# A modulated layer norm split so that its first product does not wait for the inverse root, with a re-planned instruction order, in an eight-block attention and FP4 kernel

## The chip, the cores and the metric

The kernel runs on one core of one Trainium2 chip. The metric is the device time of one execution in microseconds (us), the median of three runs. The engines are called PE (TensorE, matrix multiply; PEld is its weight load), DVE (VectorE), ACT (ScalarE), POOL (GpSimd) and SP (SyncE, which issues the DMA transfers).

## The reference

The input x has 8 batch elements of 1024 tokens by 128 features, all float32. A small table c (8x128) gives every batch element six modulation rows of 128: shift, scale and gate for the attention part (sa, ca, ga) and for the feed-forward part (sb, cb, gb).

```
mod = (silu(c) @ wmod).reshape(8, 6, 1, 128)
sa, ca, ga, sb, cb, gb = mod[:, 0], ..., mod[:, 5]
ga, gb: magnitude at least 0.25, sign kept
h = layernorm(x) * (1 + ca) + sa
x = x + ga * attn(h)
h = layernorm(x) * (1 + cb) + sb
x = x + gb * ffn(h)
```

`attn` has six layers. Each is a layer norm with weights, linear attention in 8 heads of 16 (softmax of q over the head's features, softmax of k over the tokens, context = k^T v, out = q context), a product with wo plus bias, the residual, then a second layer norm, a 128-to-512 product, a leaky ReLU, a 512-to-128 product and the residual. `ffn` is a gated unit whose three products take inputs rounded to a 4-bit grid in blocks of 16: silu(gate) * up, 128 to 352, then back to 128. `layernorm` alone, without weights, is (x - mean) / sqrt(var + 1e-5).

## The kernel before, in words

**Tiling.** One batch element is a "block" b. Its 1024 tokens lie on 128 partitions as 8 chunks of 128 features, so x of a block is a tile of 128 x 1024. Work goes by halves h of four chunks (128 x 512, one PSUM bank). Four lanes (`LANES = 4`, lane = b % 4) hold the buffers of four blocks in flight; blocks 4 to 7 take over the lanes of 0 to 3. All weights stay in SBUF.

**Order.** The kernel does not emit instructions as it describes them. [...] `Plan.order` (line 143) then plays a schedule over all engines: it takes, again and again, the step that can start earliest, ties broken by the length of the work behind it plus a "lead". Leads are set per block and stage in `LEAD` (from line 291) and altered at planned times by `TURNS` (from line 302). `LAT` (line 87) is what passes between a step's end and its readers' start on each engine, `mm`, `move`, `vec`, `act` and `pool2` (lines 217 to 243) give durations. The steps are emitted in that order, with the order on each engine fixed, so a planned duration that is off costs nothing by itself, but can place an instruction ahead of one that is ready earlier.

Into a gap of PE that the planner foresees (over `GAP` 0.6 us, half of that while it holds PE to be cold) it puts fillers, `warm` (line 1348), matmuls of the identity that nobody reads. Until `COLD` us of planned time it charges matmuls double; for a run of fillers this is decided once, at the run's start. A PSUM bank is claimed by a step only when everything is ready that any later user of the same bank needs and that was recorded before: a transpose whose eviction needs `cols` (the norm weights as columns, copied on DVE at line 515) is planned after that copy.

**The norm.** `layernorm` (line 614) is used for the plain norms of every layer (through `normed`, line 909; tiles named `_a` and `_m`) and for the two modulated norms of a block (`modulated_norm`, line 887; tiles `_i` for the first, `_f` for the second). Per half:

- four batch statistics (line 630) and four aggregates (line 636) on DVE give mean and variance (`mv`);
- ACT makes a first inverse root by Ln and Exp (lines 650, 655);
- three DVE operations of 4 elements (lines 660, 665, 670) refine it by one Newton step into `rstd`, a fourth (line 676) makes `shift` = -mean * rstd;
- the centred, scaled x is written by DVE for the first `HV` chunks (line 682, one tensor_scalar with two pointers per chunk) and by ACT for the rest (line 689, scale and bias as pointers).

`modulated_norm` calls it with HV = 2 of 4 for the first norm of a block and HV = 0 for the second, then multiplies the half by 1 + scale on DVE (line 893, one operation of 128 x 512) and adds the shift row on POOL (line 901, the same size).

What follows: the first modulated norm writes x of lane b, which the first layer's norm reads. There PE transposes the half (line 708), ACT evicts it with the norm weights (line 918) to xT, and PE multiplies it with wk (line 938) and wq (line 985). The other matmuls named below are the attention's (lines 1048, 1057, 1082, 1115), the two products of a layer's feed-forward part (lines 1161 and 1178) and those of `ffn` (line 1222 gate and up, line 1278 transposes, line 1302 down). The second modulated norm writes h, which is rounded to the grid (`fp4`, lines 736 to 781: five DVE operations, one on ACT, one on POOL) and transposed for line 1222. `w2g` (line 1130) is a POOL multiply of the last layer.

Of the kernel before, what the change touches and what calls it, by code (L numbers as in the profile page):

```python
# [83 lines left out]
class Plan:  # L84


    LAT = {"PE": 0.31, "ACT": 0.14, "DVE": 0.125, "POOL": 0.04, "SP": 2.0}
    SEE = {"PE": 0.015, "ACT": 0.0, "DVE": 0.0, "POOL": 0.1, "SP": 0.0}

    GAP, BRINK, COLD = 0.6, 0.15, 7.5  # L90
# [126 lines left out]
def vec(n):  # L217

    return 0.065 + n * 1.043e-3
# [16 lines left out]
def mm(n):  # L236

    return 0.01 + n * 1.66e-3


def move(kb):

    return max(0.45, kb * 4.0e-3)
# [6 lines left out]
def kernel(  # L250
# [53 lines left out]
        (45, [(0, 2, 1600), (3, 0, -324)]),  # L304
        (60, [(1, 1, -935)]),
        (75, [(0, 3, 1449), (1, 1, 557), (3, 1, 592)]),
        (90, [(3, 1, 2100)]),
        (120, [(3, 2, 2464), (3, 3, 2879)]),
        (135, [(0, 3, 3161)]),
        (150, [(1, 1, 2636)]),  # L310
        (165, [(1, 2, 3857)]),
        (195, [(0, 4, 1947)]),
        (210, [(1, 3, 1937)]),
        (225, [(0, 4, 2875), (0, 6, 2412), (0, 7, 99)]),
        (240, [(2, 1, -1301), (3, 3, 1394)]),
        (255, [(0, 5, 2591), (1, 3, 3015), (1, 4, -653)]),
        (270, [(3, 4, 2428)]),
        (345, [(0, 6, 2433), (4, 0, -1503)]),
        (390, [(1, 4, -2461)]),
        (405, [(3, 6, -3105)]),  # L320
        (435, [(1, 4, -3419)]),
        (450, [(3, 6, -3090)]),
        (465, [(2, 2, 551), (2, 4, -3123), (3, 6, -3105)]),
        (510, [(4, 1, -3111)]),
        (525, [(3, 6, -3271)]),
        (540, [(3, 6, -3110)]),
        (600, [(3, 7, 2098)]),
        (615, [(2, 4, -3534)]),
        (630, [(2, 6, -2208), (5, 1, 1840)]),
        (660, [(5, 1, 1745)]),  # L330
        (690, [(5, 1, 2562)]),
        (720, [(4, 3, -2144)]),
        (750, [(2, 6, -2203)]),
        (780, [(2, 6, -2201), (2, 7, -2144), (4, 3, -2142), (5, 4, -2397)]),
        (810, [(2, 7, -2186)]),
        (825, [(3, 7, -2164), (4, 3, -1269)]),
        (840, [(3, 7, -2468)]),
        (870, [(3, 7, -340)]),
        (885, [(3, 7, -553), (4, 4, 939), (4, 5, 1955)]),
        (915, [(5, 4, -1086), (6, 2, -534)]),  # L340
        (945, [(4, 6, 1221)]),
        (975, [(4, 7, -240), (7, 1, -1371)]),
        (990, [(6, 3, 282)]),
        (1005, [(4, 7, -743), (5, 4, -650)]),
        (1035, [(4, 7, -1539), (5, 5, -1458)]),
        (1050, [(5, 5, -591), (6, 3, 867), (6, 4, 1080), (7, 2, 307)]),
        (1095, [(6, 4, -754)]),
        (1110, [(6, 4, -1551)]),
        (1125, [(4, 7, -4373), (6, 4, -758)]),
        (1140, [(6, 5, -1624)]),  # L350
        (1200, [(5, 7, -1877)]),
        (1215, [(6, 5, -185), (7, 4, -2011)]),
        (1230, [(6, 5, -1795)]),
        (1245, [(6, 6, -373), (7, 5, -366)]),
        (1260, [(6, 6, -371), (7, 5, -372)]),
        (1275, [(6, 6, -365), (7, 5, -367)]),
        (1305, [(6, 7, -440), (7, 6, -443)]),
        (1320, [(7, 6, 40)]),
        (1335, [(4, 7, -2064), (5, 7, -2271), (6, 7, -2282), (7, 6, 278), (7, 7, 207)]),
# [254 lines left out]
    def layernorm(ln, dst, src, h, n, HV=HC // 2):  # L614
# [7 lines left out]
        def s(c):  # L622
            return chunks(half(src, h))[:, c, :]

        def d(c):
            return chunks(half(dst, h))[:, c, :]

        for c in range(HC):
            add(
                "DVE", 0.197, lambda c=c: nc.vector.bn_stats(stats.ap()[:, c, :], s(c)),  # L630
                r=at(src, h)[c * H // HC :][:1], w=[stats[c]],
            )

        def moments():
            for c in range(HC):
                nc.vector.bn_aggr(mv.ap()[:, c, :], stats.ap()[:, c, :])  # L636

        add("DVE", HC * 0.067, moments, r=[stats], w=[mv])
# [4 lines left out]
        def var():  # L643
# [28 lines left out]
        )  # L672

        add(
            "DVE", 0.07,
            lambda: nc.vector.scalar_tensor_tensor(z(), mean(), -1.0, y(), ALU.mult, ALU.mult),  # L676
            r=[mv, rstd], w=[shift], port=True,
        )
# [8 lines left out]
        def apply_s():  # L687
# [9 lines left out]
            w=[high] if HV else [low, high],  # L697
        )
        if HV:
            add("DVE", HV * 0.256, apply_v, r=[*at(src, h), mv, rstd], w=[low], port=True)  # L700
# [14 lines left out]
    def fp4(src, parts, ncol, n, i, last="POOL"):  # L715
# [13 lines left out]
        def each(t):  # L729
# [50 lines left out]
            last, (vec if last == "DVE" else pool2)(ncol),  # L780
# [106 lines left out]
    def modulated_norm(ln, dst, src, mod, n, name, HV):  # L887

        for h in range(H):
            layernorm(ln, dst, src, h, name, HV)  # L890
            add(
                "DVE", vec(HW),
                lambda h=h: nc.vector.tensor_tensor(
                    chunks(half(dst, h)), chunks(half(dst, h)),
                    over(mod.ap()[:, n + 1, :], HC), ALU.mult,
                ),
                r=[mod[n // 3]], w=at(dst, h), port=True,
            )
            add(
                "POOL", 1.2,  # L900
# [509 lines left out]
```

## Time and profile before

| what | us |
|---|---|
| median of 3 runs | 1406.71 |
| lowest, highest run | 1405.73, 2585.54 |
| profiled execution, its own time | 1406.12 |
| its span, first to last instruction | 1404.4 |
| granted PE clock, mean | 0.999 |

Two of the three runs are within 0.1% of each other; one took 2585.54 and does not move the median. The span leaves out 1.7 us of the profiled execution.

| stretch, us | length | PE busy | DVE busy | ACT busy | POOL busy |
|---|---|---|---|---|---|
| 0 to 50 | 50 | 44.97 | 44.06 | 33.23 | 13.15 |
| 50 to 350 | 300 | 300.00 | 229.52 | 208.56 | 36.90 |
| 350 to 400 | 50 | 48.80 | 40.08 | 35.85 | 10.54 |
| 400 to 750 | 350 | 349.88 | 287.67 | 242.37 | 59.62 |
| 750 to 800 | 50 | 48.36 | 37.96 | 29.39 | 9.27 |
| 800 to 1300 | 500 | 499.54 | 413.19 | 367.48 | 88.67 |
| 1300 to 1405 | 105 | 99.75 | 90.03 | 66.11 | 29.58 |

How to read it: busy time is the union of an engine's instructions in the stretch. Ends of matmuls are modelled and matmuls overlap, so a busy PE may still be held up for moments; the distance from one matmul's start to the next tells more. A group's mean duration is that of one instruction by itself; in a row, DVE and ACT instructions overlap, and one more costs less than the mean. An f32 matmul leaves two records, a transpose one. In a timeline row the two first numbers are the start and the length, xN is the number of instructions merged, and the bracket at the end says how long the engine had been idle before and what ended that.

### The profile page before, as it was taken

To read this page: it belongs to the slowest core of one execution; us is meant where nothing else is said; L and a number is where in the kernel's file an instruction comes from. 1 tells how busy PE (TensorE), PEld (TensorE's weight loads), DVE (VectorE), ACT (ScalarE), POOL (GpSimd) and SP (SyncE) were. 2 spreads that over 40 slices of the span, in tenths; PEclk is the share of its full clock that TensorE was granted. 3 is DMA by queue.
4 is the path that set the end of the run, shared out by engine and by line. 5 is a ranking of instruction groups with operands and counts; after the bars stand their busy time and mean duration, and the time that the engine had idled before them with its cause. 6 is when DMAs were issued, how large, how long until landed. Compare 5 with 4: busy or idle time off the path is not lost.

```text
span 1404.4 us, 26348 instructions
## 1 busy us (share of the span) xinstructions
PE 1391.3 (99%) x9181; PEld 1116.3 (79%) x9181; DVE 1142.5 (81%) x4506; ACT 983.0 (70%) x2292; POOL 247.7 (18%) x216
## 2 busy tenths in 40 slices
PE   8999999999999999999999999999999999999998
PEld 6788779688768888688788778788787787887887
DVE  8998668487798687899667899988876748879897
ACT  6777666766686686767666668876776757777774
POOL 2211001001122020312101122211210101212232
PEclk9999999999999999999999999999999999999999
DMA  7100000000000000100000000000000000000001
GB/s 218 47 1 1 2 1 1 0 1 1 17 12 16 1 2 1 42 16 13 2 0 1 16 13 16 1 16 1 1 1 1 1 1 1 2 1 1 9 17 38
DMA packets 16293, 18.79 MB, mean 13 GB/s; under 512 B 1584, under 2 KB 10392, under 8 KB 16160
## 3 DMA queue, kind: packets, MB, share of 16 engines
q1 hardware_dynamic: 16160, 17.10, 3.9%
q8 instruction: 73, 1.20, 0.4%
q14 instruction: 60, 0.49, 0.1%
HBM read 12.88 MB, written 4.22 MB: 12 GB/s over the span
## 4 chain that ended last, share of the span: by engine, by line
PE 88%; DVE 7%; ACT 2%; SPq 1%; DMA 1%; issue 1%; POOL 0%; POOLq 0%; ACTq 0%; DVEq 0%
PE ps L1178 22%; PE ps L1161 22%; PE ps L708 11%; PE ps L1048 6%; PE ps L938 5%; PE ps L1115 5%; PE ps L985 5%; PE ps L1222 5%; PE ps L1302 3%; PE ps L1278 1%; SPq L417 1%; DVE x L1100 1%; PE ps L1082 1%; PE ps L1057 1%; DMA x<-in_L_attn_x_dram 1%; DVE stats_m L630 1%
## 5 line engine op out<-in xcount | busy, mean ns | idle before, releaser
L1161 PE MATMUL ps<-xT_m,w_sb 128*128 128x512 f32 x768 | 352.0, 595 | 0.3 <-ACT xT_m L918 0.3
L1161 PEld LDWEIGHTS ps<-xT_m,w_sb 128*128 128x128 f32 x768 | 137.6, 191 | 128.8 <-issue 95.6
L1026 POOL TENSOR_TENSOR q<-q,qsum 128x512 f32<-128x512 f32 x96 | 102.4, 1075 | 709.2 <-DVE qsum L1021 377.2
L1100 DVE TENSOR_TENSOR x<-ps,x 128x512 f32<-128x512 f32 x192 | 129.7, 680 | 105.2 <-PE ps L1178 81.1
L985 PEld LDWEIGHTS ps<-wq_sb,xT_a 128*128 128x128 f32 x768 | 96.4, 192 | 26.3 <-issue 18.9
L689 ACT ACTIVATE xh_a<-x,shift_a,rstd_a 128x128 f32<-128x128 f32 x192 | 83.6, 487 | 34.6 <-DVE shift_a L676 33.4
L1115 PEld LDWEIGHTS ps<-m,qT 128*128 128x128 f32 x768 | 92.3, 192 | 11.1 <-issue 4.3
L985 PE MATMUL ps<-wq_sb,xT_a 128*128 128x128 f32 x768 | 98.8, 275 | 0.0
L1178 PEld LDWEIGHTS ps<-w_sb,hT_D 128*128 128x128 f32 x640 | 86.6, 192 | 14.3 <-issue 11.2
L938 PE MATMUL ps<-xT_a,wk_sb 128*128 128x512 f32 x192 | 96.1, 597 | 1.6 <-ACT xT_a L918 1.6
L1178 PE MATMUL ps<-w_sb,hT_C 128*128 128x128 f32 x640 | 97.6, 275 | 0.0
L1178 PE MATMUL ps<-w_sb,hT_E 128*128 128x128 f32 x640 | 97.6, 275 | 0.0
L1178 PE MATMUL ps<-w_sb,hT_B 128*128 128x128 f32 x640 | 97.6, 275 | 0.0
L1178 PE MATMUL ps<-w_sb,hT_D 128*128 128x128 f32 x640 | 97.5, 275 | 0.0
L1115 PE MATMUL ps<-m,qT 128*128 128x128 f32 x768 | 95.9, 275 | 0.1
L689 ACT ACTIVATE xh_m<-x,shift_m,rstd_m 128x128 f32<-128x128 f32 x192 | 81.8, 487 | 17.8 <-DVE shift_m L676 17.6
L1048 PEld LDWEIGHTS ps<-k,xh_a 128*128 128x128 f32 x768 | 90.4, 192 | 4.2 <-issue 2.2
L1048 PE MATMUL ps<-k,xh_a 128*128 128x128 f32 x768 | 93.4, 275 | 0.0
L650 ACT ACTIVATE rstd_a<-mv_a,eps 128x4 f32<-128x4 f32 x96 | 28.1, 296 | 88.2 <-DVE mv_a L636 84.1
L630 DVE BATCH_NORM_STATS2 stats_a<-x 128x6 f32<-128x128 f32 x384 | 84.9, 279 | 3.5 <-POOL x L901 1.7
L918 ACT ACTIVATE xT_m<-ps,cols 128x512 f32<-128x512 f32 x96 | 72.1, 776 | 20.1 <-PE ps L708 20.0
L1178 PEld LDWEIGHTS ps<-w_sb,hT_B 128*128 128x128 f32 x640 | 84.5, 192 | 1.0 <-issue 1.0
(181 smaller groups left out, 3229.8 us busy)
## 6 DMA issues: line engine op xcount, KB each, us to landing
x<-in_L_attn_x_dram SPq DMA_DIRECT2D x16, 256.0 KB, 3.4
out_dram<-x SPq DMA_DIRECT2D x14, 256.0 KB, 2.0
w_sb<-in_L_attn_w_dram SPq DMA_DIRECT2D x12, 256.0 KB, 4.4
mod<-mod_d SPq DMA_DIRECT2D x8, 256.0 KB
mod<-mod_d SPq DMA_DIRECT2D x4, 128.0 KB
out_dram<-x SPq DMA_DIRECT2D x4, 128.0 KB
wmod_b<-in_L_wmod_dram SPq DMA_DIRECT2D x1, 384.0 KB, 4.1
wk_sb<-in_L_attn_wk_dram SPq DMA_DIRECT2D x6, 64.0 KB, 4.1
```

Of the source, the lines that this page charges most:

```text
L630: "DVE", 0.197, lambda c=c: nc.vector.bn_stats(stats.ap()[:, c, :], s(c)),
L689: nc.scalar.activation(d(c), s(c), AF.Identity, bias=shift.ap()[:, c : c + 1], scale=rstd.ap()[:, c : c + 1],)
L708: nc.tensor.transpose(t.ap()[:, c * P : (c + 1) * P], chunks(half(src, h))[:, c, :], ident)
L918: lambda t=t, h=h: nc.scalar.activation(half(xT, h), t.ap(), AF.Identity, bias=col(params + 1, l), scale=col(params, l),),
L938: lambda tk=tk, h=h: nc.tensor.matmul(tk.ap(), wk_sb[:, l, :], half(xT, h), start=True, stop=True),
L985: nc.tensor.matmul(tq.ap()[:, c * D : (c + 1) * D], half(xT, h)[:, c * P : (c + 1) * P], wq_sb[:, l, :], start=True, stop=True,)
L1026: lambda h=h, hs=hs: nc.gpsimd.tensor_tensor(heads(half(q, h)), heads(half(q, h)), each(qsum.ap()[:, hs]), ALU.mult),
L1048: nc.tensor.matmul(tc_.ap()[:, :D], chunks(xh.ap())[:, c, :], chunks(k.ap())[:, c, :], start=(c == 0), stop=(c == C - 1),)
L1100: lambda: nc.vector.tensor_tensor(half(x, h), t.ap(), half(x, h), ALU.add),
L1115: nc.tensor.matmul(to.ap()[:, c * D : (c + 1) * D], half(qT, h)[:, c * P : (c + 1) * P], m.ap(), start=True, stop=True,)
L1161: lambda th=th, h=h, j=j: nc.tensor.matmul(th.ap(), w1_sb[:, l, j * P : (j + 1) * P], half(xmT, h), start=True, stop=True,),
L1178: nc.tensor.matmul(ty.ap()[:, c * D : (c + 1) * D], hidden(j)[:, c * P : (c + 1) * P], w2g.ap()[:, j, :] if l == L - 1 else w2_sb[:, l, j, :],
```

## The change

Four things change.

1. *The norm is cut in two.* `moments` ends with `rstd`; the fourth small operation (`shift`) is made only for the plain norms. These keep DVE for two chunks and ACT for two.
2. *The modulated norm has a body of its own.* Per chunk, DVE makes (x - mean) * (1 + scale) in one scalar_tensor_tensor, which needs the mean and not the inverse root. Then, in blocks whose norm is not "quick", ACT multiplies each chunk by rstd and POOL adds the shift row to the half, as before. In a quick norm, DVE multiplies by rstd and adds the shift row in a second scalar_tensor_tensor per chunk, and neither ACT nor POOL takes part. Quick are the first norm of block 0 and the second norm of block 7.
3. *Durations in the planner.* `LAT` of SP is 2.6 for 2.0, `COLD` 11.5 for 7.5, `mm` and `move` have other coefficients, and three POOL steps are longer. None of them is an instruction.
4. *Leads.* `TURNS` is a new table of 53 rows for 57; `LEAD` is kept.

```diff
-    LAT = {"PE": 0.31, "ACT": 0.14, "DVE": 0.125, "POOL": 0.04, "SP": 2.0}
+    LAT = {"PE": 0.31, "ACT": 0.14, "DVE": 0.125, "POOL": 0.04, "SP": 2.6}
...
-    GAP, BRINK, COLD = 0.6, 0.15, 7.5
+    GAP, BRINK, COLD = 0.6, 0.15, 11.5
...
-    return 0.01 + n * 1.66e-3
+    return 0.0115 + n * 1.654e-3
...
-    return max(0.45, kb * 4.0e-3)
+    return max(0.45, kb * 3.6e-3)
...
-        (45, [(0, 2, 1600), (3, 0, -324)]),
-        (60, [(1, 1, -935)]),
...
+        (45, [(0, 2, 1600)]),
+        (60, [(1, 1, -1561)]),
...
-    def layernorm(ln, dst, src, h, n, HV=HC // 2):
+    def moments(ln, src, h, n, shifted=False):
...
-        add(
-            "DVE", 0.07,
-            lambda: nc.vector.scalar_tensor_tensor(z(), mean(), -1.0, y(), ALU.mult, ALU.mult),
-            r=[mv, rstd], w=[shift], port=True,
-        )
+        if shifted:
+            add(
+                "DVE", 0.07,
+                lambda: nc.vector.scalar_tensor_tensor(
+                    z(), mean(), -1.0, y(), ALU.mult, ALU.mult
+                ),
+                r=[mv, rstd], w=[shift], port=True,
+            )
+        return mv, rstd, shift
+
+    def layernorm(ln, dst, src, h, n):
+
+
+        HV = HC // 2
+        mv, rstd, shift = moments(ln, src, h, n, True)
...
-            last, (vec if last == "DVE" else pool2)(ncol),
+            last, vec(ncol) if last == "DVE" else pool2(ncol) * 1.15,
...
-    def modulated_norm(ln, dst, src, mod, n, name, HV):
+    def modulated_norm(ln, dst, src, mod, n, name, quick):
+
+
 
         for h in range(H):
-            layernorm(ln, dst, src, h, name, HV)
-            add(
-                "DVE", vec(HW),
-                lambda h=h: nc.vector.tensor_tensor(
-                    chunks(half(dst, h)), chunks(half(dst, h)),
-                    over(mod.ap()[:, n + 1, :], HC), ALU.mult,
-                ),
-                r=[mod[n // 3]], w=at(dst, h), port=True,
-            )
-            add(
-                "POOL", 1.2,
-                lambda h=h: nc.gpsimd.tensor_tensor(
-                    chunks(half(dst, h)), chunks(half(dst, h)),
-                    over(mod.ap()[:, n, :], HC), ALU.add,
-                ),
-                r=[mod[n // 3]], w=at(dst, h),
-            )
+            mv, rstd = moments(ln, src, h, name)[:2]
+
+            def chunk(t, c, h=h):
+                return chunks(half(t, h))[:, c, :]
+
+            def first(cs, chunk=chunk, mv=mv):
+                for c in cs:
+                    nc.vector.scalar_tensor_tensor(
+                        chunk(dst, c), chunk(src, c), mv.ap()[:, c, 0:1],
+                        mod.ap()[:, n + 1, :], ALU.subtract, ALU.mult,
+                    )
+
+            def second(cs, chunk=chunk, rstd=rstd):
+                for c in cs:
+                    nc.vector.scalar_tensor_tensor(
+                        chunk(dst, c), chunk(dst, c), rstd.ap()[:, c : c + 1],
+                        mod.ap()[:, n, :], ALU.mult, ALU.add,
+                    )
+
+            def scaled(cs, chunk=chunk, rstd=rstd):
+                for c in cs:
+                    nc.scalar.mul(chunk(dst, c), chunk(dst, c), rstd.ap()[:, c : c + 1])
+
+            Q = HC // H
+            for q, (s, d) in enumerate(zip(at(src, h), at(dst, h))):
+                cs = range(q * Q, (q + 1) * Q)
+                add(
+                    "DVE", Q * vec(D), lambda f=first, cs=cs: f(cs),
+                    r=[s, mv, mod[n // 3]], w=[d], port=True,
+                )
+                if quick:
+                    add(
+                        "DVE", Q * vec(D), lambda f=second, cs=cs: f(cs),
+                        r=[rstd, mod[n // 3]], w=[d], port=True,
+                    )
+                else:
+                    add("ACT", Q * act(D, 1), lambda f=scaled, cs=cs: f(cs), r=[rstd], w=[d])
+            if not quick:
+                add(
+                    "POOL", 1.3,
+                    lambda h=h: nc.gpsimd.tensor_tensor(
+                        chunks(half(dst, h)), chunks(half(dst, h)),
+                        over(mod.ap()[:, n, :], HC), ALU.add,
+                    ),
+                    r=[mod[n // 3]], w=at(dst, h),
+                )
...
-                "POOL", pool2(NJ * D) + 0.1,
+                "POOL", pool2(NJ * D) + 0.28,
...
-                    "POOL", pool2(HW) + 0.2,
+                    "POOL", pool2(HW) + 0.33,
...
-        modulated_norm(ln, hq, x, mod, 3, f"f{b}", 0)
+        modulated_norm(ln, hq, x, mod, 3, f"f{b}", b == B - 1)
...
-        modulated_norm(ln, x, x0s[b], mod, 0, f"i{b}", HC // 2)
+        modulated_norm(ln, x, x0s[b], mod, 0, f"i{b}", b == 0)
```

## The prediction

> **What bounds the kernel now.** I read the page's busy shares first, then the busy time of the engines by stretch, then the same table for the filler matmuls alone, then the timeline around the places where TensorE is not busy.
>
> ```profile
> PE 1391.3 (99%) x9181; PEld 1116.3 (79%) x9181; DVE 1142.5 (81%) x4506; ACT 983.0 (70%) x2292; POOL 247.7 (18%) x216
> ...
> PE   8999999999999999999999999999999999999998
> ```
>
> TensorE (PE) is busy for 1391.3 of 1404.4 us. The next engine, VectorE (DVE), has 262 us free. So only two things can shorten the run: less work on TensorE, or fewer moments in which it waits. Part of its busy time is no work of the reference: the planner puts "warm" matmuls (line 1350) into gaps that it foresees. By stretch, those alone (us of window, PE busy and count, PEld busy and count, granted clock, DMA):
>
> ```profile
> 0.00:50.00 50.00, 15.23 (x112) 14.17 (x112) 1.00 0.61 185
> 50.00:1300.00 1250.00, 0.00 (x0) 0.00 (x0) 1.00 0.02 6
> 1300.00:1350.00 50.00, 0.61 (x4) 0.53 (x4) 1.00 0.02 6
> 1350.00:1405.00 55.00, 7.78 (x58) 7.11 (x58) 0.99 0.10 35
> ```
>
> There are 174 records, which is 87 fillers (an f32 matmul leaves two records). Fillers mark waiting at both ends of the run; between 50 and 1300 us there is none. I also took, over the timeline's TensorE records, what each start-to-start distance has over the usual one of its shape (0.429 us for 512 columns, 0.112 for 128, 0.109 for a transpose, 0.296 for 352). That sums to 6.3 us before 50 us, 7.8 between 50 and 1300, and 3.5 after. So the span is
>
> 1404.4 = 1358.2 work + 23.8 fillers (by start distances) + 17.6 hidden or open waits + 1.6 before the first matmul + 3.2 after the start of the last.
>
> All that a better order could ever win is 46.2 us (3.3%), and most of that is unavoidable: the first data must land, the last block must drain.
>
> How a wait in the middle comes about is seen in the largest one (start, length, instruction):
>
> ```profile
> 791.36 1.32 POOL L1130 TENSOR_TENSOR w2g<-w_sb,mod 128x512 f32<-128x512 f32 x1 [12.37 <-DVE shift_m L665]
> 791.36 1.34 DVE L670 SCALAR_TENSOR_TENSOR rstd_m<-shift_m,rstd_m 128x4 f32<-128x4 f32 x2
> 792.62 1.29 POOL L901 TENSOR_TENSOR h<-h,mod 128x512 f32<-128x512 f32 x1
> ...
> 792.70 1.30 DVE L676 SCALAR_TENSOR_TENSOR shift_m<-mv_m,rstd_m 128x4 f32<-128x4 f32 x2
> 793.92 1.11 DVE L682 TENSOR_SCALAR xh_m<-x,mv_m,rstd_m 128x128 f32<-128x128 f32 x4
> ...
> 794.31 1.68 PE L708 MATMUL ps<-ident,xh_m 128*128 128x128 f32 x8 [1.25 <-DVE xh_m L682]
> ```
>
> A pair of 4-element operations that elsewhere takes 0.23 us takes 1.34 and 1.30, exactly as long as a GpSimd multiply and then the modulation's GpSimd add run. VectorE finishes xh_m late, and TensorE idles 1.25 us. And it costs more than that:
>
> ```profile
> 792.00:796.00 4.00, 2.68 (x18) 1.82 (x16) 4.00 (x10) 2.04 (x5) 1.90 (x2) 1.00 0.00 0
> 796.00:800.00 4.00, 3.68 (x5) 1.62 (x6) 3.81 (x21) 1.56 (x4) 0.00 (x0) 0.57 0.00 0
> ```
>
> The granted clock is 0.57 in the next 4 us: four records of 512 columns start 0.85 us apart and not 0.43, 1.7 us more. The whole place costs 4.1 us of the 7.8.
>
> **The change part by part.** *TensorE work.* None is added or removed. Counted from the two built instruction streams by operation and shape, the matmuls agree except for the fillers: 87 before, 56 after. Loads and stores are the same 103.
>
> *The norm with modulation, engine by engine.* It runs for 2 halves of 16 norms. VectorE loses 32 multiplies of 512 (line 893, 0.68 us alone, 0.60 in a row: 19.2 us), 32 tensor_scalar of 128 (line 682: four in 1.10, one in 0.34, so 0.25 each: 8 us) and 32 of the 4-element shifts (line 676, about 0.10 in a row: 3.2 us), 30.4 us in all. It gains 144 scalar_tensor_tensor of 128 elements with one pointer. No row shows that operation on two SBUF tensors. Lower bound: batch statistics of the same length (0.87 for four, 0.28 for one: 0.20 each); upper bound: the two-pointer tensor_scalar, 0.25. I take 0.25, since both have pointers. That makes 36 us (28.8 at the lower bound), a net +5.6 us (-1.6 to +5.6) on an engine with 262 us free. [...] ScalarE loses 96 applications (line 689, four in 1.64, one in 0.49: 0.38 each, 37 us) and gains 112 scalings with one pointer (nearest row: line 607, one pointer, 0.40 alone, 0.09 under line 689's 0.49 with two; so between 0.29 and 0.38 in a row): 33 to 43 us, on an engine with 420 us free. Its table loads go from 31 to 33, 2.6 us more. GpSimd loses 4 adds of 1.27. In the middle, then, the edit is worth nothing by itself; what hides it is TensorE's own queue of ready work. If that cover is gone, one half's norm comes up to 0.4 us later (1.0 against 0.60).
>
> *The start.* Block 0's norm now runs on VectorE alone. Ahead of the first transposes there stand 23 fillers instead of 41, and 35 instead of 56 in the whole start. At the spacing of the big batch below (82 records in 9.32 us, 0.227 per filler) that would be 4.8 us. I don't book it, since a filler that is gone can become idle time:
>
> ```profile
> 11.67 9.32 PE L1350 MATMUL warm<-ident 128*128 128x128 f32 x82
> ...
> 19.70 0.86 ACT L689 ACTIVATE xh_a<-x,shift_a,rstd_a 128x128 f32<-128x128 f32 x2
> 20.28 0.18 DVE L515 COPY cols<-ps 128x24 f32<-128x24 f32 x1
> 20.83 1.04 PE L708 MATMUL ps<-ident,xh_a 128*128 128x128 f32 x8
> 21.46 1.45 ACT L918 ACTIVATE xT_a<-ps,cols 128x512 f32<-128x512 f32 x2 [0.29 <-PE ps L708]
> ```
>
> Both halves of xh_a are ready by 20.6 us, and the eviction to xT_a needs `cols` (20.46). In the changed stream the work that stands on VectorE ahead of that copy is 32 batch statistics (0.197), 32 aggregates (0.073), 20 small operations (0.085) and 28 of 128 elements (0.25), 17.3 us; before, the same kinds and two multiplies gave 13.3. The copy is queued behind lane 2's norm, which was behind it before. So with the same 2.3 us of waits `cols` comes at about 24, not 20.3, the 23 fillers (which the planner charges double, as their run starts before 11.5 us) end at about 16.9, and TensorE idles some 5 us around two transposes, long enough to lose the clock. On the other side, up to the first xh_m VectorE has 33.1 us of work against 33.4 before, and it is what sets this stage (busy 29.94 of 30 us between 20 and 50); and TensorE has done 22.05 us of work when the first matmul of line 1161 comes, against 20.05. So the start is worth -2.0 us; bounds -6 (the fillers' 4.8 and some of the 6.3 us of waits) and +4 (the late copy in full).
>
> *The end.* The last block's norm loses the GpSimd add (1.27 to 1.86 us per half, on the chain to the last gate matmuls) for four VectorE pieces (1.0). Fillers go from 31 to 21. Here the order behind the last gate matmuls is nearly the old one, so I book them: 10 x 0.227 = -2.3 us; bounds 0 and -5.
>
> *The middle.* Durations and leads only reorder. The waits there, 7.8 us, were not foreseen before (no filler stands there), and the new order will have its own. A stall of that kind costs 1.3 (one at 382 us, clock kept) to 4.1 us. I take one large one less than before, half believed: -2 us; bounds -6 and +8 (two more large ones).
>
> Sum against the profiled span: 1404.4 - 2.0 - 2.3 - 2.0 = 1398.1. That execution took 1406.12, and the median of the runs is 1406.71, 2.3 above the span: 1400.4.
>
> **A rule on the clock.** [...] The row above shows it halved after two idle gaps of 1.25 and 0.34 us with transposes between them. [...] I keep the row for the upper bound.
>
> **The rivals.**
> 1. The waits move but don't go (1405 to 1414): `cols` is late by its full 4 us and a new stall or two appear in the middle, so that 4 + 4 eats the 4.3 to 6.3 of gain: about 1408. For it: VectorE is busy 48.97 of 50 us from 50 to 100, where a late start isn't made up. Against: TensorE is never idle from 47 to 380 us before.
> 2. Slower: norms late at VectorE behind GpSimd, over and over. The place is every half whose first new operation (two SBUF tensors) meets a GpSimd multiply, as at 791 us. At 4.1 us each, with -4.3 at the ends, the time passes 1406.7 + 28 from (28 + 4.3)/4.1 = 8 such stalls on. Ten would give 1443. Against: before, one in 1250 us, and the slack in the middle is large.
> 3. Much faster: all 7.8 us of the middle, and the bounds of both ends, -6 and -5, plus the waits after 1300: 1406.7 - 7.8 - 6 - 5 - 3.5 = 1384; over 2% (below 1378.6) it would need the first data to come earlier too, which nothing does.
> 4. The modulation edit does nothing and only the order acts: the same as the forecast without the end's 2.3, 1402.7; it lies in the same range and is told apart by experiment only.
>
> **How the numbers follow.** The forecast with rival 4: 0.70, 1400.4, its own range 1391 to 1406. Rival 1: 0.24. Rival 2: 0.03, rival 3: 0.03, of which a third or so beyond 2%. To hold 8 in 10 I take 1390.0 to 1410.0: most of the forecast's case and the nearer half of rival 1. Beyond 2%, about what a measurement of this kernel can tell from no change, lie 0.02 on the fast side and 0.04 on the slow side (rival 2 and a worse start); 0.94 is within.
>
> **What would show it.** Right: TensorE again 99% busy with 56 fillers (112 records); first xT_a eviction at 24 us or later with idle TensorE before it; first matmul of line 1161's group no later than 47 us or with 2 us more work behind it; total waits in the middle 4 to 8 us; VectorE's and ScalarE's busy time within 10 us of before; the new operations at 0.25 in a row. Wrong: a granted clock under 0.9 in several slices of the middle, or a start that reaches dense TensorE work only after 50 us.

## The result, and the profile after

| | before | after |
|---|---|---|
| median of 4 runs, us | 1406.22 | 1417.55 |
| lowest to highest | 1405.22 to 2585.54 | 1417.10 to 1418.41 |
| ratio, 95% interval | | 1.0088 [1.0076, 1.0101] |
| span of the profiled execution | 1404.4 | 1415.8 |

The changed kernel is slower by 0.9%, by less than 2% but well outside its interval; the forecast was 0.4% faster (1400.4, range 1390 to 1410). The ratio leaves out the one execution of before that took 2585.54 us. The page of after:

```profile
PE 1391.3 (98%) x9119; PEld 1110.4 (78%) x9119; DVE 1150.7 (81%) x4554; ACT 980.4 (69%) x2310; POOL 244.9 (17%) x212
...
PE   7999999999999999999999999999999999999998
```

TensorE is busy for the same 1391.3 us in a span that is 11.4 us longer. Only the first of the 40 slices has lost a digit, so most of the loss lies in stretches too short for this view. The fillers alone, by stretch, as they were shown of before (us of window, PE busy and count, PEld busy and count, clock, DMA):

```profile
0.00:50.00 50.00, 10.85 (x70) 9.95 (x70) 0.93 0.54 164
50.00:1300.00 1250.00, 0.00 (x0) 0.00 (x0) 1.00 0.02 7
1300.00:1350.00 50.00, 0.00 (x0) 0.00 (x0) 1.00 0.00 1
1350.00:1416.00 66.00, 5.83 (x42) 5.24 (x42) 1.00 0.09 33
```

56 fillers, as built. The start-to-start distances, taken as in the prediction, give 1415.8 = 1359.0 work + 16.9 fillers + 35.0 waits + 4.9 at the two ends: 6.9 us of fillers less, 17.4 us of waits more. By stretch (the differences are taken before rounding):

| us of fillers + waits | 0 to 50 | 50 to 100 | 100 to 1300 | 1300 to end |
|---|---|---|---|---|
| before | 16.0 + 6.3 | 0 | 7.8 | 7.8 + 3.5 |
| after | 11.7 + 10.9 | 6.0 | 11.9 | 5.2 + 6.3 |
| difference | +0.3 | +6.0 | +4.1 | +0.1 |

So fillers became idle time at both ends, one for one, and 10.1 us of waits are new between 50 and 1300. Three places show how.

*The start*, from after's timeline (start, length, instruction; the bracket gives the idle time before it and what ended it):

```profile
21.43 2.44 ACT L920 ACTIVATE x<-x,rstd_i 128x128 f32<-128x128 f32 x8 [1.98 <-DVE rstd_i L663]
22.70 0.16 DVE L511 COPY cols<-ps 128x24 f32<-128x24 f32 x1
22.96 0.55 PE L576 MATMUL ps<-cols,wv_sb 128*128 128x1 f32 x2 [3.56 <-issue]
23.78 0.47 ACT L643 ACTIVATE rstd_i<-mv_i,eps 128x4 f32<-128x4 f32 x2
24.16 1.43 ACT L956 ACTIVATE xT_a<-ps,cols 128x512 f32<-128x512 f32 x2
24.97 3.60 PE L976 MATMUL ps<-xT_a,wk_sb 128*128 128x512 f32 x4 [0.39 <-ACT xT_a L956]
27.08 0.69 DVE L983 TENSOR_REDUCE nmax<-ps 128x1 f32<-128x512 f32 x1 [0.87 <-PE ps L976]
```

TensorE idles before 22.96, and the granted clock from 24 to 28 us is 0.50: four records of 512 columns take 3.60 us. `cols` comes at 22.70, but the eviction follows only at 24.16: on ScalarE it stands behind eight scalings of block 2. The same four records before, and then the first matmul of the feed-forward group in before (line 1161) and in after (line 1199):

```profile
22.30 1.98 PE L938 MATMUL ps<-xT_a,wk_sb 128*128 128x512 f32 x4 [0.32 <-ACT xT_a L918]
...
46.93 3.27 PE L1161 MATMUL ps<-xT_m,w_sb 128*128 128x512 f32 x7
...
49.77 7.03 PE L1199 MATMUL ps<-xT_m,w_sb 128*128 128x512 f32 x16
```

*From 50 to 100 us*, from the same timeline:

```profile
49.44 1.40 DVE L906 SCALAR_TENSOR_TENSOR x<-x,mv_i,mod 128x128 f32<-128x128 f32 x2
49.57 1.12 POOL L1064 TENSOR_TENSOR q<-q,qsum 128x512 f32<-128x512 f32 x1 [13.59 <-ACT xT_m L956]
51.94 3.40 DVE L906 SCALAR_TENSOR_TENSOR x<-x,mv_i,mod 128x128 f32<-128x128 f32 x6
52.17 1.20 POOL L1064 TENSOR_TENSOR q<-q,qsum 128x512 f32<-128x512 f32 x1 [1.47 <-DVE qsum L1059]
53.33 1.33 POOL L1168 TENSOR_TENSOR w2g<-w_sb,mod 128x512 f32<-128x512 f32 x1
57.55 1.27 POOL L939 TENSOR_TENSOR x<-x,mod 128x512 f32<-128x512 f32 x1 [2.89 <-ACT x L920]
58.87 0.87 DVE L621 BATCH_NORM_STATS2 stats_a<-x 128x6 f32<-128x128 f32 x4 [3.10 <-POOL x L939]
61.46 0.68 DVE L621 BATCH_NORM_STATS2 stats_a<-x 128x6 f32<-128x128 f32 x3 [0.99 <-POOL x L939]
```

Two things happen to block 3's first norm. Six pieces of the new product take 3.40 us beside GpSimd's multiplies, where four take 1.11 elsewhere (0.26 each). Then VectorE stands idle for 3.10 and 0.99 us until GpSimd has added the shift row. TensorE has long runs of lines 1199 and 1216 meanwhile and doesn't wait; its waits come afterwards (PE, PEld, DVE, ACT, POOL busy, clock, DMA):

```profile
60.00:70.00 10.00, 9.14 (x67) 7.67 (x66) 9.01 (x57) 6.53 (x21) 2.50 (x2) 1.00 0.01 2
70.00:80.00 10.00, 8.65 (x53) 6.23 (x52) 10.00 (x25) 8.56 (x21) 2.39 (x2) 1.00 0.00 0
80.00:90.00 10.00, 9.03 (x75) 8.13 (x74) 10.00 (x45) 8.04 (x22) 4.36 (x4) 1.00 0.01 2
```

VectorE is full from 70 us on, and TensorE falls to 8.65. Before, TensorE is at 10.00 in each of these windows; the middle one:

```profile
70.00:80.00 10.00, 10.00 (x80) 8.97 (x79) 10.00 (x26) 8.64 (x21) 2.06 (x2) 1.00 0.01 2
```

How much of these waits answers to the held pieces and to the idle time is what e6 and e15 test.

*The middle.* Before's stall at 791 us is gone, and one like it has come at 637:

```profile
634.74 1.39 POOL L788 TENSOR_TENSOR g<-fv_g,scale_g 128x704 f32<-128x704 f32 x1 [11.28 <-DVE fv_g L780]
634.75 1.39 DVE L653 SCALAR_TENSOR_TENSOR shift_a<-mv_a,rstd_a 128x4 f32<-128x4 f32 x1
...
637.09 1.39 POOL L788 TENSOR_TENSOR g<-fv_g,scale_g 128x704 f32<-128x704 f32 x1 [0.97 <-DVE shift_a L658]
...
637.15 1.35 DVE L663 SCALAR_TENSOR_TENSOR rstd_a<-shift_a,rstd_a 128x4 f32<-128x4 f32 x1
...
639.27 0.89 PE L715 MATMUL ps<-ident,xh_m 128*128 128x128 f32 x4 [1.35 <-DVE xh_m L690]
```

The four largest waits of after between 100 and 1300 us, by start distances, stand near 515 (1.7 us), 606 (1.3), 637 (3.1) and 1017 (1.3). Within 3 us ahead of each, an operation of VectorE (or a pair) took 1.1 to 1.4 us beside a GpSimd multiply: a pair of pieces of a plain norm's xh_m (1.34 at 515.30), a 32-element operation of `fp4` (1.21 at 603.17), the 4-element one above (1.35), and one piece of the new product (1.16 at 1016.50). Only the place at 637 was tested (e6).

### The profile page after: what moved, and what is told of

It reads as the page before. It is cut to its first block, busy times and chain, and to the rows that moved or that the text cites. A ratio compares the mean times of both kernels' runs of the same rounds, so it can differ in the third digit from the quotient of the medians.

```text
span 1415.8 us, 26220 instructions
## 1 busy us (share of the span) xinstructions
PE 1391.3 (98%) x9119; PEld 1110.4 (78%) x9119; DVE 1150.7 (81%) x4554; ACT 980.4 (69%) x2310; POOL 244.9 (17%) x212
## 4 chain that ended last, share of the span: by engine, by line
PE 75%; DVE 19%; ACT 4%; issue 1%; POOL 1%; DMA 0%; SPq 0%; POOLq 0%; DVEq 0%; ACTq 0%
PE ps L1199 20%; PE ps L1216 20%; PE ps L715 9%; PE ps L1153 5%; PE ps L1086 4%; PE ps L976 4%; PE ps L1023 4%; PE ps L1260 4%; PE ps L1340 2%; DVE x L1138 2%; DVE nmax L983 1%; DVE qmax L1032 1%; DVE stats_m L621 1%; PE ps L1316 1%; DVE x L906 1%
## 5 line engine op out<-in xcount | busy, mean ns | idle before, releaser
L1216 PEld LDWEIGHTS ps<-w_sb,hT_D 128*128 128x128 f32 x640 | 86.2, 192 | 11.9 <-issue 10.3
L999 ACT ACTIVATE kT<-ps,nmax 128x512 f32<-128x512 f32 x96 | 65.1, 684 | 41.1 <-DVE nmax L990 40.9
L697 ACT ACTIVATE xh_m<-x,shift_m,rstd_m 128x128 f32<-128x128 f32 x192 | 81.6, 487 | 17.1 <-DVE shift_m L669 16.6
L1260 PE MATMUL ps<-wguT,hTf 128*128 128x352 f32 x256 | 85.0, 463 | 1.6 <-ACT hTf L1238 0.7
```

What stands on the lines that cost most here:

```text
L697: nc.scalar.activation(d(c), s(c), AF.Identity, bias=shift.ap()[:, c : c + 1], scale=rstd.ap()[:, c : c + 1],)
L1216: nc.tensor.matmul(ty.ap()[:, c * D : (c + 1) * D], hidden(j)[:, c * P : (c + 1) * P], w2g.ap()[:, j, :] if l == L - 1 else w2_sb[:, l, j, :],
L1260: lambda t=t, cc=cc, n=n: nc.tensor.matmul(t.ap()[:, :I], hT.ap()[:, cc * P : (cc + 1) * P], wguT[:, n, :], start=True, stop=True,),
```

## The experiments

The theories after the result: (A) TensorE loses where VectorE comes late, because GpSimd holds it or because the new norm makes it wait; (B) the order lost something and the norm is innocent; (C) the queue in front of the first evictions delays everything. The ratio is to before on the same chip. W is the sum of TensorE's waits by start distances in the profiled execution.

| run | us | ratio to before [95%] | span | fillers | W | W 50 to 100 | W 100 to 1300 |
|---|---|---|---|---|---|---|---|
| e1: before's order, new norm | 1433.38 | 1.0200 [1.0185, 1.0215] | 1431.1 | 24.0 | 45.2 | 2.5 | 28.4 |
| e2: after's order, old norm | 1439.71 | 1.0243 [1.0228, 1.0258] | 1437.7 | 20.0 | 56.0 | 5.5 | 28.1 |
| e3: after, copy to `cols` early | 1418.51 | 1.0094 [1.0079, 1.0109] | 1417.4 | 21.3 | 34.3 | 6.2 | 12.1 |
| e4: after, fillers at the start | 1421.16 | 1.0114 [1.0097, 1.0131] | 1418.6 | 26.6 | 29.2 | 6.1 | 12.1 |
| e5: after, evictions early in the list | 1417.97 | 1.0090 [1.0075, 1.0105] | 1417.1 | 20.7 | 34.6 | 6.4 | 12.0 |
| e6: after, six GpSimd multiplies on VectorE | 1415.19 | 1.0069 [1.0054, 1.0084] | 1412.9 | 16.8 | 32.4 | 4.9 | 10.5 |
| e7: e1, first product later | 1427.50 | 1.0161 [1.0146, 1.0176] | 1429.3 | 26.5 | 41.0 | 6.1 | 18.1 |
| e8: before, the two quick norms only | 1408.90 | 1.0022 [1.0013, 1.0031] | 1407.5 | 24.4 | 20.2 | 0 | 6.9 |
| e9: after, whole start group early | 1419.56 | 1.0104 [1.0089, 1.0119] | 1416.9 | 17.3 | 37.5 | 6.4 | 12.1 |
| e10: e9 and e6 | 1415.07 | 1.0074 [1.0057, 1.0091] | 1413.4 | 16.9 | 34.4 | 4.6 | 10.5 |
| e11: before, five GpSimd operations on VectorE | 1401.73 | 0.9978 [0.9969, 0.9987] | 1399.4 | 23.2 | 14.1 | 0 | 4.7 |
| e12: before, one planned latency changed | 1489.76 | 1.0605 [1.0589, 1.0621] | 1488.0 | 75.9 | 50.3 | 0 | 34.1 |
| e13: e9, block 0's chain first | 1420.95 | 1.0109 [1.0092, 1.0126] | 1419.5 | 16.7 | 40.6 | 6.4 | 11.8 |
| e14: e13 and e6 | 1417.25 | 1.0086 [1.0071, 1.0101] | 1416.2 | 16.6 | 37.3 | 4.6 | 10.3 |
| e15: after, block 3's first norm quick | 1417.46 | 1.0088 [1.0071, 1.0104] | 1415.8 | 16.9 | 35.2 | 4.2 | 13.4 |
| e16: e15 and e6 | 1414.66 | 1.0066 [1.0051, 1.0081] | 1412.6 | 16.7 | 32.3 | 4.2 | 10.5 |

**e1 and e2: norm and order crossed.** e1 plans before's order with the old norm's steps and emits the new norm in their places; e2 does the reverse on after.

```diff
+        n0 = planned("DVE", 0.07, r=[mv, rstd], w=[shift], port=True)
+        n1 = planned("ACT", (HC - HV) * (act(D, 2) + 0.04), r=[*at(src, h), shift, rstd], w=to)
...
+        n3 = planned("POOL", 1.2, r=[row[k // 3]], w=at(dst, h))
...
+            real.add((n0, 1), lambda cs=cs: first(cs), [a, mv, row[k // 3]], [b])
...
+                real.add((n1, 1), lambda cs=cs: scaled(cs), [rstd], [b])
```

> The order of before is kept on every engine, matmul for matmul; only the modulated norm is the new one, its first product in the place of the old small shift, its ACT scaling in the place of the old application, quick in blocks 0 and 7. If the re-planned order is what costs (my theory): 1404 to 1408 us, within 2 us of before. If the new norm itself costs: 1411 us or more. If the new norm is a gain that the order ate: under 1403.

> The mirror of it: the order of the changed kernel, with the old norm (ACT and DVE apply, DVE multiplies the half, POOL adds) in its places. Order theory: it stays slow, 1415 to 1422 us, and the start is a little later still, since block 0 needs the POOL add again. Norm theory: back to 1411 or less.

e1 fell into the case that the norm itself costs, e2 into neither of its two. e1 is 28 us slower than before, e2 22 us slower than after: an order and a norm fit each other, and theory (B) can't be decided this way. e1's waits of VectorE show one reason that the prediction had not looked for (waited for; us in total, times, longest):

```profile
DVE x L788 <- DMA out_dram<-x: 10.1, 4, 4.5
...
DVE h L788 <- PE ps L1263: 7.1, 5, 2.3
```

The new first product needs only the mean, so it writes its destination earlier; the destination was still being stored or read.

**e7: the first product later.**

```diff
-real.add((n0, 1), lambda cs=cs: first(cs), [a, mv, row[k // 3]], [b])
-real.add((n1, 1), lambda cs=cs: scaled(cs), [rstd], [b])
+real.add((n1, 1), lambda cs=cs: first(cs), [a, mv, row[k // 3]], [b])
+real.add((n1, 2), lambda cs=cs: scaled(cs), [rstd], [b])
```

> Before's order with the new norm, as in the first experiment, but with the first product placed where ScalarE's application of the old norm stood (it was placed at the old shift operation, as early as it could be). In the first experiment VectorE waited 10.1 us for output transfers that still read the buffer (longest 4.5) and 7.1 for matmuls of line 1263's group. Theory that the 28 us came from the product's early write into a buffer still in use: those waits fall below 2 us and the time to 1405 to 1412. Rival, that the new norm's longer way (VectorE, ScalarE, GpSimd) doesn't fit into before's order wherever it is put: 1420 to 1435.

The wait for the output fell to 0.8 us, the one for line 1263 below the listed 0.7, and W from 100 to 1300 us from 28.4 to 18.1; the time only to 1427.5, in the rival's range. The early write is one cost of the cross, not the main one. Of the largest stalls left, those at 52.6, 651 and 803 to 806 us have a 1- or 4-element operation held 1.2 us by GpSimd; the one at 873 has eight pieces in a row, 3.20 us, ahead of the mask of the context (line 1176).

**e8: the quick norms alone.** Before's order; the new norm only in block 0's first and block 7's second norm.

```diff
+            if quick:
+                layernorm(ln, dst, src, h, name, HV, (mod, n, quick))
+                continue
```

> Before's order; the new norm only where it is quick, that is in block 0's first and block 7's second, all other norms as before. Left at before's time (1403 to 1408) if the quick form is worth nothing at either end; 1400 to 1403 if taking ScalarE and GpSimd out of both ends brings what I had booked there; 1408 to 1412 if VectorE, which has 3 us more work in the start, sets the pace there.

1408.9, at the lower edge of the slower case: the end gets 0.5 us more fillers and 2.5 us more waits, the start 1.0 more waits. In before's order, whose leads were searched for the old norm, the quick form alone is a small loss at both ends.

**e3, e4, e5, e9: the start of after.** e3 moves the copy to `cols` ahead of block 2's first product. e4 puts 21 fillers behind the two transposes. e5 moves the evictions too, but the transposes stand behind block 2's scalings in the list, so the evictions stayed behind these (23.80 us). e9 moves the whole group.

```diff
+    order.remove(mark["cols"])
+    order.insert(order.index(mark["first", "i2"]), mark["cols"])
...
+        i = order.index(mark["turned", h]) + 1
+        order[i:i] = [filler] * n
...
+    i = 1 + max(j for j, s in enumerate(order) if getattr(s, "n", -1) in deps)
+    order[i:i] = [copy, *group, *both]
```

> The changed kernel with one instruction moved: the copy of cols on DVE goes ahead of block 2's first new products, everything else stays in order. Theory of the start (the copy stands behind another block's norm, and PE goes idle and loses its clock behind it): first matmul of line 976's kind at about 20.5 us and not 24.97, clock 1.0 between 24 and 28, span 3 to 6 us shorter, 1411.5 to 1414.5 us. Rival (DVE sets the pace of the start whatever comes first): within 1 us of the changed kernel, 1416.5 to 1418.5.

> The changed kernel with 21 fillers more on PE, 5 behind the first half's transposes and 16 behind the second's, where it idles for 1.3 and 3.8 us; nothing else moves. If the lost clock is what costs at the start: four records of 512 at 0.43 and not 0.85 us, 1.5 to 2.5 us faster, 1415 to 1416 us. If the clock is only a companion of a start that DVE sets: 1417 to 1418, and the same waits between 60 and 90 us.

> After, but the copy to cols (VectorE) and the two evictions to block 0's first xT_a (ScalarE) stand ahead of block 2's first product and its eight scalings. Theory that the start is late because these evictions are queued on ScalarE behind those scalings: first matmul of the wk group at 20.5 to 21.5 instead of 24.97, granted clock above 0.9 from 24 to 28, span 3 to 6 us shorter than after's 1415.8 (1410 to 1413). Rival, that VectorE's own work sets the pace up to the first feed-forward matmul (49.77 in after) whatever comes before: that matmul stays at 49 or later and the span shrinks by under 1 us.

> After, and this time the whole group stands ahead of block 2's first product and scalings on its engines: the copy to cols (VectorE), the fillers and the eight transposes of block 0's first layer (TensorE, same order on it), and the two evictions to xT_a (ScalarE). In the run before, the evictions still stood behind the scalings. Theory that ScalarE's queue makes the start late: first matmul of the wk group at 20 to 21 instead of 24.97, clock kept, first feed-forward matmul 2 to 4 us earlier than after's 49.77, span 1411 to 1414. Rival, that VectorE's work up to the first feed-forward sets the pace: that matmul at 49 or later, span 1415 to 1417.

None gains. e4 kept the clock at 1.00, but its fillers, all in one PSUM bank, ran 0.53 us apart and not 0.23, and the first matmul of the wk group (line 976 of after) came at 28.79, 3.8 us later than in after; so e4 doesn't tell what the lost clock alone costs. e9 decides against (C). Its timeline:

```profile
18.91 1.43 ACT L959 ACTIVATE xT_a<-ps,cols 128x512 f32<-128x512 f32 x2
...
20.35 3.11 PE L980 MATMUL ps<-xT_a,wk_sb 128*128 128x512 f32 x4
...
26.77 0.68 DVE L987 TENSOR_REDUCE nmax<-ps 128x1 f32<-128x512 f32 x1
...
29.58 1.10 PE L717 MATMUL ps<-ident,kT 128*128 128x128 f32 x4 [3.47 <-ACT kT L1003]
```

The matmuls start 4.6 us earlier, the row maximum that follows them on VectorE only 0.3, and TensorE idles 3.47 us there instead; the first feed-forward matmul comes at 49.95 (49.77 in after). Ahead of it, the transposes of xh_m start at 47.27 after 1.14 us of waiting for VectorE's subtraction of the row maximum (line 1043), as in after (47.08, line 1039, 1.14 us).

**e13: block 0's chain first on VectorE.** e9, with block 2's first norm behind block 0's row maxima and subtractions.

```diff
+    late = [
+        s for s in order[i:j]
+        if getattr(s, "stage", None) in ((2, 0), (2, 1)) and s.eng in ("DVE", "ACT", "POOL")
+    ]
+    order[i:j] = [s for s in order[i:j] if s not in late] + late
```

> After with the start group early as in the ninth run, and block 2's first norm (its first product, small operations, scalings, GpSimd adds and the statistics that follow) behind block 0's first row maxima and subtractions on VectorE, ScalarE and GpSimd; TensorE's order is after's. Theory that VectorE's order sets the start (2.2 us of the new product and some 2 us of block 2's statistics stand ahead of block 0's row maximum): that maximum at 22 to 24 instead of 27.08, first feed-forward matmul at 45 to 47 instead of 49.77, span 2 to 4 us shorter than after. Rival, that block 2 is then late instead, since its second operand is needed at 36 us already: first feed-forward matmul at 49 or later, span within 1 us of after's or longer.

The row maximum came at 22.44, as the theory had it, and the first feed-forward matmul at 53.01, as the rival had it: now a copy of block 0 on ScalarE stands behind block 2's moved scalings (TensorE idles 7.09 us until 35.33). Every hand-made shift moved the wait to another in-order queue. That the start can't be shorter isn't shown.

**e6, e10, e14: GpSimd out of VectorE's way.** Six GpSimd multiplies run on VectorE in the same place, in after, in e9's and in e13's kernel.

```diff
+        on[0] = nc.vector if step in moved else nc.gpsimd
         step.fn()
```

> After, but six GpSimd multiplies run on VectorE in the same place of the order: the three at 49.57, 52.17 and 53.33 and the one at 78.54 us (each ran beside pieces of the new first product that took 1.14 to 1.38 us instead of 0.35), and the two of 704 columns at 634.74 and 637.09 (beside 4-element operations that took 1.39 and 1.35). Theory that VectorE is held while GpSimd runs: the held pieces go back to 0.35, the waits of TensorE from 50 to 100 us fall from 6.0 to 3 to 4, those from 600 to 650 from 4.3 to 1 to 3; span 3 to 5 us shorter than after. Rival, that these waits are only the late start handed on and the order's own: VectorE gets 0.6 to 0.9 us more for each, waits unchanged or up by 1 to 2, span the same or 2 us longer.

> After with both edits: the start group early, and the six GpSimd multiplies on VectorE. If the two causes are separate, the gain is the sum of both alone: 2.9 us from the multiplies (measured) and what the start group brings, so a span of 1409 to 1411. If the late start and the stalls from 50 to 100 us are one delay that can be won only once, 1412 to 1413.

> The run before and the six GpSimd multiplies on VectorE. If start and stalls are separate causes: 2.9 us (measured for the multiplies alone) below the run before it. If a shorter start only turns into longer waits from 50 to 100 us: the same as with the multiplies alone, a span of 1413.

The six pieces that took 3.40 us in after, in e6:

```profile
51.34 0.52 DVE L906 SCALAR_TENSOR_TENSOR x<-x,mv_i,mod 128x128 f32<-128x128 f32 x2
51.78 0.68 DVE L1064 TENSOR_TENSOR q<-q,qsum 128x512 f32<-128x512 f32 x1
52.38 1.13 DVE L906 SCALAR_TENSOR_TENSOR x<-x,mv_i,mod 128x128 f32<-128x128 f32 x4
```

e6 is 2.9 us shorter in span (2.4 in the medians), just short of the 3 to 5 expected: W falls by 1.1 from 50 to 100 us and by 1.6 at 600 to 650 (4.3 to 2.8). In e10 and e14 the same gain (3.5 and 3.3 us in span, 4.5 and 3.7 in the medians) appears on top of the start's own result, a loss of 1.1 and of 3.7. Holding is a cause of its own, worth some 3 us of the 11.4.

**e15, e16: VectorE's idle time.** In after (and in e6's kernel) block 3's first norm is quick too.

```diff
+                    f = second if name == "i3" else scaled
-                    add("ACT", Q * act(D, 1), lambda f=scaled, cs=cs: f(cs), r=[rstd], w=[d])
+                    add("ACT", Q * act(D, 1), lambda f=f, cs=cs: f(cs), r=[rstd], w=[d])
```

> After, with block 3's first norm quick as well: its eight scalings (ScalarE, 55.72 to 60.1 us) and two adds (GpSimd, 57.55 and 60.16) become eight second products on VectorE in the place of the scalings; TensorE's order is after's. Theory that VectorE's idle 4.1 us before 61.5, spent waiting for those adds, come back as TensorE's waits from 60 to 90: block 3's statistics start at 57.9 and 58.7 instead of 58.87 and 61.46, waits from 50 to 100 us 3 to 4.5 instead of 6.0, span 1.5 to 3 us shorter. Rival, that VectorE is simply full in this stretch: it has 2.1 us more to do, and waits and span stay within 0.7 us.

> The run before with the six GpSimd multiplies on VectorE as well (2.9 us shorter alone). If idle time and holding are separate losses, they add up: waits from 50 to 100 us 2 to 3.5, span 1409 to 1411.5. If both are the same slack, 1412 to 1413.

e15's statistics start at 57.70, the idle 4.1 us are gone although VectorE has 2.1 us more to do, and W from 50 to 100 falls from 6.0 to 4.2. The span didn't follow: at 637 the stall cost 1.4 us more, since TensorE lost its clock there (0.62 from 638 to 642 us, 1.00 in after). With the moved multiplies (e16) W from 50 to 100 is 4.2 again and not 2 to 3.5.

The clock hides part of these gains. From 70 to 80 us it is 1.00 in after and 0.83 in e6, e15 and e16; e6's row:

```profile
70.00:80.00 10.00, 8.65 (x45) 6.15 (x44) 9.30 (x23) 7.29 (x17) 2.38 (x2) 0.83 0.00 0
```

Records at about twice their usual distance make up 1.1 us of W from 50 to 100 in e6, 1.7 in e15 and 1.9 in e16, against 0.2 in after. Without them, as an estimate from the start distances, 5.8 us in after become 3.7 in e6, 2.5 in e15 and 2.3 in e16. By these figures both causes act, the idle time more than the holding, and they overlap: they are mostly the same slack of VectorE. The last 2.3 us were not won by any edit, and little of it reached the time: in the medians e15 gains 0.1 us on after, e16 0.5 us on e6.

**e11: the same cause in before.** Old norm, before's order; w2g at 39.52, 42.89, 380.52, 791.36 us and the add at 792.62 run on VectorE and later: the first two at 95.68 and 97.94, the others at 385.58, 793.85 and 793.26. The edit is e6's with other steps.

> Before, old norm, with five GpSimd operations on VectorE and a little later there: the multiplies w2g at 39.52, 42.89, 380.52 and 791.36 us and the add at 792.62. They held operations of VectorE for 0.9 to 1.3 us each, at 382 and 791 us with TensorE waiting (1.66 and 4.4 us). Theory that VectorE is held while GpSimd runs on SBUF operands: both stalls go, span 4 to 6 us shorter (1398 to 1400.5), time 1400 to 1402. Rival, that the norm at 791 is late on its own: the stall stays at 3 us or more and the time within 2 us of before.

```profile
789.50 0.23 DVE L673 SCALAR_TENSOR_TENSOR rstd_m<-shift_m,rstd_m 128x4 f32<-128x4 f32 x2
...
789.87 1.11 DVE L685 TENSOR_SCALAR xh_m<-x,mv_m,rstd_m 128x128 f32<-128x128 f32 x4
...
791.04 1.04 PE L711 MATMUL ps<-ident,xh_m 128*128 128x128 f32 x8
```

The pair that took 1.34 us takes 0.23 and the stall is gone. W from 100 to 1300 us falls from 7.8 to 4.7. The span is 5.0 us shorter than in before's profiled execution; the median on the same chip falls by 3.0 us (0.2%). At 1401.73 it is faster than both kernels.

**e12: how far an order holds.**

```diff
-    LAT = {"PE": 0.31, "ACT": 0.14, "DVE": 0.125, "POOL": 0.04, "SP": 2.0}
+    LAT = {"PE": 0.31, "ACT": 0.14, "DVE": 0.125, "POOL": 0.04, "SP": 2.1}
```

> Before with one planned number changed: the latency of a DMA is 2.1 instead of 2.0 us in the planner, no instruction is added or changed but the fillers, and the leads are not looked for anew. If the leads fit only the plan they were looked for in, the order degrades: 150 or more fillers and 1425 to 1460 us. If the order is robust against such a change: 1403 to 1412 us.

1489.76, beyond the expected 1425 to 1460: a twentieth more in one planned latency, leads kept, costs 6%, with 288 fillers for 87. In this case the leads did not carry over to a changed plan. So two plans also differ by how well the search for their leads turned out, which has nothing to do with what was changed.

## Why the prediction was wrong, step by step

- *TensorE's work, fillers, durations: right.* Work 1359.0 against 1358.2, 56 fillers. The new operation takes 0.26 in a row: the price from the row (0.25) held, and the lower bound from the batch statistics (0.20) was too low. VectorE is busy 8.2 us longer (5.6 forecast), ScalarE 2.6 less; eight scalings take 2.44 us, one 0.40, so each further one 0.29: the lower end.
- *The start, booked -2.0, measured +0.3 up to 50 us.* What it named came: fillers end at 16.6 (16.9), `cols` at 22.7 (24), idle time of 3.6 us and a lost clock (0.50 from 24 to 28 us), the first xh_m on VectorE at 44.55 (44.52 before). The step that failed is the credit for TensorE's extra 2.05 us of work by the first matmul of the feed-forward group: "no later than 47 us or with 2 us more work behind it" came as 49.77, 2.8 us later with 2 us more work, so the credit was eaten; though xh_m was on time, its transposes waited 1.14 us for VectorE and started at 47.08. Its queue was incomplete, too: it named VectorE's ahead of `cols`, while ScalarE's held the eviction (e5, e9) and VectorE's the row maximum after it (e9).
- *The middle, booked -2 (bounds -6 and +8), measured +10.1.* This is the step that made the sign. It said that "the edit is worth nothing by itself; what hides it is TensorE's own queue of ready work", and that without this cover one half's norm comes up to 0.4 us late. The cover was taken from before's trace, where TensorE never waits from 50 to 380 us. But VectorE had no room there (48.97 of 50 us busy, a figure that stood under rival 1). In the new form ScalarE's scaling and GpSimd's add both follow the root, VectorE stood idle for 4.1 us for them, and five pieces held by GpSimd cost it 4.5 more (1.14, 1.15, 1.38, 1.37, 1.16 against 0.35). TensorE waited 6.0, of which e6, e15 and e16 give more than half back (5.8 to 2.3, the estimate without the lost clock). The other 4.1 us, net: before's stalls at 382 and 791 are gone, and those near 515, 606, 637 and 1017 are new, one of them beside a piece of the new product. That these come with the order is argued, not shown; whether a new search for leads would avoid them wasn't tried.
- *The end, booked -2.3, measured +0.1.* Ten fillers went (-2.6), waits rose by 2.7. The prediction refused this credit in the start, because "a filler that is gone can become idle time", and took it at the end. e8 shows waits, not gain, from the quick norm there.
- *The rivals.* Rival 1 (waits move, about 1408) had the sign, but 1.3 us in the place of 11; it named the right stretch (50 to 100 us, where VectorE is full) and the wrong cause, since an earlier `cols` gained nothing in e3 and e9. Rival 2 named one of the mechanisms, first products held by GpSimd: 8 of 144 pieces were, for 7.4 us of VectorE in all. It priced each at 4.1 us of TensorE; five of them lie in the stretch where e6 won 1.1 us of waits.
- *The clock.* In after it was at 0.50 from 24 to 28 us, behind an idle window of 3.56 us. In e9 it was at 0.65 from 20 to 24 us, behind idle gaps of 0.19 and 1.34 us with transposes between them; the four records of 512 columns from 20.35 took 3.11 us (1.98 in before). That is like the row of before that was kept for the bound (0.57 behind 1.25 and 0.34 us). But gaps of 1.35 and 0.81 us at 639 to 641 us in after, also with transposes between them, and one of 1.14 us at 383 us in before left it at 1.00. What decides between these cases no run here tells.

The part that stays open is how much of the 11.4 us is the norm's and how much the search's. e1, e7 and e2 show that neither can be exchanged alone, and e12 that a badly fitting order costs over 80 us. The planner's new durations and the new leads were not tried apart from the norm. With both of the shown causes reduced (e16), the span is still 8.2 us longer than before's.

## What to carry to other kernels

Ask of every wait that a change shortens which engine is full just behind it: here TensorE's cover hid a late producer only while its run of ready work lasted, and the producer had no slack afterwards to catch up. A filler that disappears is a gain only where the work behind it comes earlier by a chain that is followed through every in-order queue. Where leads were searched for one plan, take GpSimd work off VectorE's way at the stalls one by one before planning anew; in e11 that was worth 3 us.

## What the runs showed of the hardware

VectorE's scalar_tensor_tensor, tensor_scalar and tensor_tensor with all operands in SBUF were looked at where they started at least 0.01 us after a GpSimd tensor_tensor that had over 0.15 us still to run. They ended with it or after it in 48 of 48 cases before and in 57 of 63 after. In the other 6 a run of such VectorE operations was already under way when the GpSimd operation started, and it was the GpSimd operation that took longer (2.18 for 1.27 us, 2.62 for 1.39). Batch statistics, aggregates, reductions, reciprocals and whatever read PSUM were not held once (429 cases before, 405 after, none over 0.03 us beyond the median of its like). A 4-element operation waited as long as one of 128 elements (1.35 at 637.15, 1.38 at 53.44), so the size doesn't matter here and the form does. The prediction had seen the effect at 791 us and priced it per stall of TensorE, and not per piece of a product of which it put 144 on VectorE. Beyond the median of the same operation, the held operations of VectorE took 30.1 us before, 38.7 after and 25.3 in e11.
